# The border to the experts: fills of empty rows beside the puts, on two queues, the plan in memory of its own, weights ahead of rows

## The chip, the cores and the metric

The kernel runs on one core of a Trainium2 chip. The metric is the device time of one execution in microseconds (us). Engines are named as in the profile: PE (matrix products and transposes; PEld its weight loads), DVE, ACT, POOL (elementwise engines; POOL also issues the indirect DMAs) and SP (issues DMAs and computes nothing). An engine that issues a DMA does it in its own stream of instructions, in order; such rows carry a q (SPq, ACTq).

## The reference

A tensor x of 2 x 256 x 48 x 48 passes two layers. The first is a mix of local attention and convolutions. The second turns the picture into 2 x 2304 tokens of 256 numbers and runs a state-space token mixer, and behind it a mixture of experts. All is float32. The part that matters here is the mixture:

```python
xf = x.reshape(-1, D)
gate_logits = xf @ Wg + bg
top_w, top_i = jax.lax.top_k(gate_logits, TOP_K)          # 2 of 8 experts for each token
top_w = jax.nn.softmax(top_w, axis=-1)
w_dense = jnp.sum(jax.nn.one_hot(top_i, E, dtype=xf.dtype) * top_w[..., None], axis=1)
for e in range(E):
    h = jax.nn.gelu(xf @ W1[e] + b1[e], approximate=False)  # 256 -> 1024
    out = out + w_dense[:, e:e + 1] * (h @ W2[e] + b2[e])   # 1024 -> 256
```

and the result is added to the tokens (after their normalization, for the experts' input).

## The kernel before, in words

The kernel doesn't run all tokens through all experts. It sorts them: `xs` is a table in device memory with one part for each of the 8 experts (`PART` = 4608 + 256 rows) and a spare piece behind them. A row has 265 numbers: the token's 256 channels, its weights for the experts, and its number.

**The tail of the mixer.** While the mixer runs (`mamba`), each group of up to six chunks of 128 tokens is routed: DVE finds the two best experts and, from running counts, the row of each token in each expert's part. POOL then puts the rows: two indirect DMAs of 128 rows for a chunk, 72 in all (`put`, line 1630, `xs<-u,rows`). They are declared free of order among themselves, as a group named "rows". The last group's counts end in `self.taken`, one number for each expert. The order on PE, DVE, ACT and SP in this stage is written out by a planner (`Flow`) in the program; POOL's follows from the same plan.

**The border** (`experts`). `ends` (line 1730) is `taken` plus one: the first empty row of each part. `fill(e)` (line 1747) writes 256 rows of zeros with the number of a spare token there, since the experts work on tiles of 128 or 256 rows and the last tile of a part reaches past its tokens. The row is a register's value, loaded on the issuing engine by `value` (line 1711). `plan` (lines 1641 to 1708) works out on DVE, in some forty small instructions, which expert and which row each tile has. `fetch(i)` loads tile i: its rows `ex` (line 1758 for tile 0, line 1764 for others), the biases `bt` (line 1767) and the weights `wt` of 2 MB (line 1769). Tile 0 is always the first of expert 0, whose weights are loaded long before (`first_weights`). All these DMAs are issued by SP.

**The tiles.** There are 36 pair tiles of 256 rows and 4 single tiles of 128 that always run, and 4 more under a condition. For each: `turn` transposes the rows on PE (line 896, copied out on DVE, line 898) and takes out the weights of the tokens and their numbers; `up` makes the first product (line 1826) in eight chunks, each in one of four PSUM banks, with a Gelu on ACT (line 1830); `down` makes the second product, for pair tiles with seven products instead of eight (line 1864), for which `weight_sums` (lines 1800 to 1803, `ts`) and `hidden_sums` (lines 1812 to 1815, `ss`) make sums on DVE; `finish` scales the result on ACT and adds it to `acc` by an indirect DMA of POOL (line 1836). `run` goes over the tiles; at the end of tile i it fetches tile i + 3.

Outside the planner's part a scheduler of the framework orders the instructions of each engine when the program is built; what is wrapped in `keep_in_program_order` keeps its order. It also sets the waits: an instruction waits for every earlier one that it may conflict with in memory, unless both were declared free of order. Memory of a closed pool is given to later pools; the pools of `experts`, that of the plan among them, lie where the mixer's were.

Of the kernel before, what the change touches and what calls it, by code (L numbers as in the profile page):

```python
# [31 lines left out]
F32 = mybir.dt.float32  # L32
I32 = mybir.dt.int32
AF = mybir.ActivationFunctionType
# [3 lines left out]
P = 128  # L38
B, C, H, W = 2, 256, 48, 48
N = H * W  # L40
NH = C // P
# [29 lines left out]
E, HID = 8, 1024  # L71
NHC = HID // P

TR = 256
# [4 lines left out]
NROWS = E * PART + TR  # L79
XW = C + E + 1  # L80
WMAT = NH * HID + NHC * C
# [144 lines left out]
class Kernel:  # L226
# [1496 lines left out]
    def experts(self, ctx):  # L1723
        nc, ins = self.nc, self.ins
        self.psum(ctx, 4, 2)
        hp = self.pool("eh", 2, ctx)
        ew = self.pool("ew", 3, ctx)
        plan = self.pool("plan", 1, ctx)
        ends = plan.tile([P, E], I32, name="ends")
        nc.vector.tensor_scalar(ends, self.taken, 1.0, None, ALU.add)  # L1730
        sp = [mybir.EngineType.SP]
        fetched, turned, hidden, sums = {}, {}, {}, {}

        tiles = []

# [5 lines left out]
        usual = len(tiles)  # L1741
        tiles += [(1, i) for i in range(NUSUAL, NSINGLE)]

        def fill(e):
            row = self.value(ends[0:1, e : e + 1], sp, NROWS - TR)
            put = self.tc.keep_in_program_order(
                nc.sync.dma_start(
                    self.expert_rows(self.xs[bass.ds(row, TR), :]), self.none
                )
            )  # L1750
            self.tc.declare_no_dep(put.ins, group="fill", reason="every part of the table has its own")
            self.tc.add_to_no_dep_group("fill", put.ins)

        def fetch(i):
            halves, n = tiles[i]
            x = hp.tile([P, 2, XW], F32, tag="ex", name="ex", bufs=3)[:, :halves]
            if i == 0:
                self.tc.keep_in_program_order(nc.sync.dma_start(x, self.expert_rows(self.xs[0:TR, :])))
                fetched[i] = x, self.first_weights[:, :WMAT], self.first_weights[:, WMAT:]
                return  # L1760
            at = where[2 - halves]
            row = self.value(at[0:1, 0, n : n + 1], sp, NROWS - TR)
            part = self.value(at[0:1, 1, n : n + 1], sp, (E - 1) * P)
            nc.sync.dma_start(x, self.expert_rows(self.xs[bass.ds(row, halves * P), :]))

            bt = hp.tile([P, WCOL - WMAT], F32, tag="bt", name="bt", bufs=5)
            self.tc.keep_in_program_order(nc.sync.dma_start(bt, ins["We"][bass.ds(part, P), WMAT:]))
            wt = ew.tile([P, WMAT], F32, tag="wt", name="wt")
            self.tc.keep_in_program_order(nc.sync.dma_start(wt, ins["We"][bass.ds(part, P), :WMAT]))
            fetched[i] = x, wt, bt  # L1770

        def turn(i):

            halves = tiles[i][0]
            x, wt, bt = fetched[i]
            xt = hp.tile([P, NH, halves * P], F32, tag="ext", name="ext")
            self.transposes(
                xt.rearrange("p k q -> p (k q)"),
                [x[:, j, k * P : (k + 1) * P] for k in range(NH) for j in range(halves)], nc.vector.tensor_copy,
            )  # L1780
            own = hp.tile([P, halves, E], F32, tag="own", name="own")
            nc.vector.tensor_tensor(
                own, x[:, :, C : C + E], bcast(bt[:, NHC + C :], 1, [P, halves, E]), ALU.mult
            )
            weight = hp.tile([P, halves], F32, tag="weight", name="weight")
            nc.vector.tensor_reduce(weight, own, AX.X, ALU.add)
            token = hp.tile([P, halves], I32, tag="token", name="token", bufs=12)
            nc.vector.tensor_copy(token, x[:, :, XW - 1].bitcast(I32))
            turned[i] = xt, weight, token

        def weight_sums(i):


            if i >= len(tiles) or tiles[i][0] == 1:
                return
            w2 = fetched[i][1][:, NH * HID : NH * HID + NHC * C].rearrange("p (k h o) -> p k h o", k=NHC, h=2)
            b11, b12, b21, b22 = (w2[:, k * NHC // 2 : (k + 1) * NHC // 2, h] for k in range(2) for h in range(2))
            ts = hp.tile([P, 4, NHC // 2, P], F32, tag="ts", name="ts", bufs=1)
            t1, t2, t3, t4 = (ts[:, j] for j in range(4))
            nc.vector.tensor_sub(t1, b12, b11)  # L1800
            nc.vector.tensor_sub(t3, b22, b12)
            nc.vector.tensor_sub(t2, b22, t1)
            nc.vector.tensor_sub(t4, b21, t2)
            sums[i] = dict(b11=b11, b21=b21, b22=b22, t1=t1, t2=t2, t3=t3, t4=t4)
# [11 lines left out]
            sums[i] |= dict(a11=a11, a12=a12, a22=a22, s1=s1, s2=s2, s3=s3, s4=s4)  # L1816

        def up(i):
            rows = tiles[i][0] * P
            xt, wt, bt = turned[i][0], *fetched[i][1:]  # L1820
            w1 = wt[:, : NH * HID].rearrange("p (k o) -> p k o", k=NH)
            hid = hidden[i] = hp.tile([P, NHC, rows], F32, tag="hid", name="hid")
            for c in range(NHC):
                ps = self.bank()
                for k in range(NH):
                    nc.tensor.matmul(  # L1826
                        ps[:, :rows], lhsT=w1[:, k, c * P : (c + 1) * P], rhs=xt[:, k, :],
                        start=k == 0, stop=k == NH - 1,
                    )
                nc.scalar.activation(hid[:, c, :], ps[:, :rows], AF.Gelu, bias=bt[:, c : c + 1])  # L1830

        def finish(i, y, j):

# [6 lines left out]
            self.tc.add_to_no_dep_group(f"tile{i}", put.ins)  # L1840

        def down(i):
            wt, bt, hid = *fetched[i][1:], hidden[i]
            w2 = wt[:, NH * HID : NH * HID + NHC * C].rearrange("p (k o) -> p k o", k=NHC)
            b2 = bt[:, NHC : NHC + C]
            banks = self.ps2.tile([P, 2, 512], F32, tag="banks", name="po")
            if tiles[i][0] == 1:
                y = hp.tile([P, C], F32, tag="ey", name="ey", bufs=5)
                po = banks[:, 0, :C]
                for c in range(NHC):  # L1850
                    nc.tensor.matmul(po, lhsT=hid[:, c, :P], rhs=w2[:, c, :], start=c == 0, stop=c == NHC - 1)  # L1851
                nc.vector.tensor_add(y, po, b2)
                finish(i, y, 0)
            else:
                v = sums.pop(i)
                p = {}

                for n, (name, a, w) in enumerate((
                    (1, "a11", "b11"), (7, "s3", "t3"), (2, "a12", "b21"), (4, "a22", "t4"), (5, "s1", "t1"),
                    (6, "s2", "t2"), (3, "s4", "b22"),  # L1860
                )):
                    p[name] = banks[:, n // 4, n % 4 * P : (n % 4 + 1) * P]
                    for c in range(NHC // 2):
                        nc.tensor.matmul(p[name], lhsT=v[a][:, c], rhs=v[w][:, c], start=c == 0, stop=c == NHC // 2 - 1)  # L1864
                y0, y1 = (hp.tile([P, C], F32, tag="ey", name="ey", bufs=5) for _ in range(2))
                p1, u2, u3, u4 = (hp.tile([P, P], F32, tag=f"u{j}", name=f"u{j}", bufs=1) for j in range(4))
                add = nc.vector.tensor_add
                nc.scalar.copy(p1, p[1])  # L1868
                add(y0[:, :P], p[2], p1)
                add(u2, p[6], p1)  # L1870
                add(u3, p[7], u2)
                add(u4, p[5], u2)
                add(y1[:, :P], p[4], u3)
                add(y1[:, P:], p[5], u3)
                add(y0[:, P:], p[3], u4)
                for j, y in enumerate((y0, y1)):
                    add(y, y, b2)  # L1877
                    finish(i, y, j)
            del fetched[i], turned[i], hidden[i]

        fill(0)
        fetch(0)
        where, many = self.plan(plan)
        turn(0)
        for e in range(1, E):
            fill(e)
        fetch(1)
        fetch(2)
        weight_sums(0)

        def run(first, end):
            for i in range(first, end):
                up(i)
                if i + 1 < end:
                    turn(i + 1)
                if tiles[i][0] == 2:
                    hidden_sums(i)
                down(i)
                if i + 1 < end:
                    weight_sums(i + 1)  # L1900
                if i + 3 < end:
                    fetch(i + 3)
# [39 lines left out]
    def run(self):  # L1942
# [30 lines left out]
            self.layer0(l0)  # L1973
        up = self.pool("route", 1)
        self.taken = up.tile([P, E], F32, name="taken")
        nc.vector.tensor_copy(self.taken, self.c["base"])
        self.first_weights = self.pool("ew0", 1).tile([P, WCOL], F32, name="wt")
        nc.sync.dma_start(self.first_weights, self.ins["We"][0:P, :])
# [93 lines left out]
```

## Time and profile before

| | us |
|---|---|
| runs of before | 1396.8, 1399.08, 1402.14, 1402.41, 1402.56 |
| median | 1402.14 |
| the profiled execution | 1399.72 |
| its span (first to last instruction) | 1397.9 |
| PE busy | 1261.5 (90%) |
| DVE busy | 1015.5 (73%) |
| ACT busy | 789.3 (56%) |
| POOL busy | 531.6 (38%) |
| last put of rows begins | 826.21 |
| first product of tile 0 begins | 839.42 |
| first product of tile 1 begins | 857.67 |

Every time below is counted from the begin of the span. In a chain of waits a row has its start, its length and what ran; in a timeline a bracket gives the idle time of the engine before the instruction and what ended it. A row such as "SPq L1747 <- DMA ex<-xs: 1.9, 1, 1.9" says that SP's stream stood before line 1747 for 1.9 us in all, once, at the longest 1.9 us, until a DMA of `ex<-xs` landed.

### The profile page before, as it was taken

The page shows a single profiled execution, that of the slowest core. Times are in us where ns is not written, and L with a number is a line of the kernel's source. Part 1 is how long each engine was busy: PE and PEld are TensorE (multiplying, and loading weights), DVE is VectorE, ACT ScalarE, POOL GpSimd, SP SyncE. Part 2 cuts the span into 40 slices and gives each one's busy share as a digit, 9 for nine tenths or more (in the row PEclk, how much of TensorE's full clock was granted, in tenths as well). Part 3 has the DMA queues.
Part 4 walks back from the last instruction along what each step waited for, and adds up shares of the span by engine and source line. Part 5 has one row for each costly group of instructions (what it writes and reads, how often), then busy time and mean ns, then how long its engine had stood idle before and what let it go on. Part 6 is the DMA issues. An engine that isn't in the chain of part 4 may idle for free.

```text
span 1397.9 us, 23793 instructions
## 1 busy us (share of the span) xinstructions
PE 1261.5 (90%) x8144; PEld 1006.3 (72%) x8144; DVE 1015.5 (73%) x2638; ACT 789.3 (56%) x1932; POOL 531.6 (38%) x648
## 2 busy tenths in 40 slices
PE   4999999997999889898988709999999999999993
PEld 3566767666676566665656508999999999999992
DVE  5999999998789879799988635665565566556552
ACT  2688878887987676776876403333332333333332
POOL 4313030111366777868676840212221221222220
PEclk9999999998999999999999859999999999999997
DMA  8321313112323232333242128767665775676637
GB/s 287 105 92 44 122 59 106 37 55 75 105 66 96 85 102 90 117 92 124 82 129 88 54 94 289 230 184 235 211 217 178 239 233 181 217 235 207 188 81 278
DMA packets 101259, 199.55 MB, mean 143 GB/s; under 512 B 10491, under 2 KB 83788, under 8 KB 95692
## 3 DMA queue, kind: packets, MB, share of 16 engines
q1 hardware_dynamic: 83756, 171.57, 36.1%
q0 software_dynamic: 14400, 19.74, 7.3%
q10 hardware_dynamic: 2980, 6.69, 1.2%
q8 instruction: 66, 1.08, 0.3%
q14 instruction: 57, 0.47, 0.1%
HBM read 158.71 MB, written 44.18 MB: 145 GB/s over the span
## 4 chain that ended last, share of the span: by engine, by line
PE 51%; DVE 12%; DMA 4%; ACT 2%; POOL 2%; issue 2%; SPq 1%; another core or an unknown queue 0%; DVEq 0%; ACTq 0%; POOLq 0%
PE bank L1826 18%; PE po L1864 16%; PE bank L910 4%; PE zbank L910 2%; PE bank L1421 2%; PE bank L1403 2%; DVE xc L1107 2%; PE bank L1360 1%; POOL xs L1630 1%; PE bank L896 1%; DVE mt L1323 1%; DVE bc L1107 1%; PE po L1851 1%; PE bank L1341 1%; DMA cz<-bc 1%
## 5 line engine op out<-in xcount | busy, mean ns | idle before, releaser
L1836 POOL DMA_INDIRECT acc<-ey,token x76 | 118.7, 1561 | 422.4 <-ACT ey L1835 380.1
L1826 PE MATMUL bank<-ext,wt 128*128 128x256 f32 (+1 forms) x1280 | 271.5, 371 | 3.4 <-DMA wt<-in_We 2.6
L1826 PEld LDWEIGHTS bank<-ext,wt 128*128 128x128 f32 x1280 | 232.3, 191 | 32.5 <-DVE ey L1877 2.7
L1830 ACT ACTIVATE hid<-bank,bt 128x256 f32<-128x256 f32 (+1 forms) x312 | 143.2, 461 | 93.3 <-PE bank L1826 88.3
L1868 ACT COPY u<-po 128x128 f32<-128x128 f32 x36 | 9.6, 266 | 225.1 <-PE po L1864 225.1
L1864 PE MATMUL po<-ts,ss 128*128 128x128 f32 x864 | 108.2, 275 | 0.0
L1864 PEld LDWEIGHTS po<-ts,ss 128*128 128x128 f32 x864 | 102.3, 192 | 0.0
L586 DVE SCALAR_TENSOR_TENSOR x<-hid,w2r,x 128x1128 f32<-128x1128 f32 (+3 forms) x72 | 99.9, 1392 | 0.4 <-ACT hid L580 0.2
L910 PE MATMUL bank<-xn,win 128*128 128x387 f32 x240 | 94.7, 518 | 1.2 <-DVE lg L1446 1.0
L675 POOL COPY kp<-kp 128x10 f32<-128x10 f32 (+1 forms) x60 | 23.5, 392 | 189.0 <-DVE kp L668 189.0
L794 ACT ACTIVATE prob<-prob,top 128x308 f32<-128x308 f32 x144 | 78.1, 548 | 17.5 <-DVE top L783 17.1
L1315 ACT ACTIVATE mt<-mt,cum 128x128 f32<-128x128 f32 x288 | 87.4, 396 | 0.0
L1107 DVE SCALAR_TENSOR_TENSOR xc<-bank,vec,xc 128x384 f32<-128x384 f32 x144 | 85.1, 606 | 1.9 <-ACT xc L1096 1.7
L1800 DVE TENSOR_TENSOR ts<-wt 128x512 f32<-128x512 f32 x36 | 24.9, 692 | 81.2 <-PE po L1864 81.2
L1813 DVE TENSOR_TENSOR ss<-hid 128x512 f32<-128x512 f32 x36 | 24.9, 691 | 77.8 <-ACT hid L1830 77.8
L1630 POOL DMA_INDIRECT xs<-u,rows x72 | 71.9, 998 | 22.5 <-issue 16.7
L910 PE MATMUL zbank<-xn,win 128*128 128x384 f32 x192 | 75.8, 518 | 4.2 <-ACT z L1217 4.2
L1864 PE MATMUL po<-wt,hid 128*128 128x128 f32 x576 | 76.1, 275 | 0.0
L1421 PE MATMUL bank<-wout,y 128*128 128x264 f32 x288 | 72.4, 395 | 2.4 <-DVE ss L1436 1.9
L1864 PEld LDWEIGHTS po<-wt,hid 128*128 128x128 f32 x576 | 70.1, 192 | 0.1
L825 PE MATMUL bank<-pt,val 110*64 110x128 f32 (+1 forms) x864 | 69.4, 278 | 0.8 <-ACT pt L815 0.8
L800 ACT ACTIVATE prob<-prob,rden 128x308 f32<-128x308 f32 x144 | 67.7, 546 | 4.1 <-DVE rden L849 4.0
(293 smaller groups left out, 3010.1 us busy)
## 6 DMA issues: line engine op xcount, KB each, us to landing
wt<-in_We SPq DMA_DIRECT2D x39, 2048.0 KB
mt<-decays SPq DMA_DIRECT2D x36, 512.0 KB
ex<-xs SPq DMA_DIRECT2D x36, 265.0 KB
rd<-decays SPq DMA_DIRECT2D x68, 128.0 KB
val<-vtab SPq DMA_DIRECT2D x72, 110.0 KB
bt<-in_We SPq DMA_DIRECT2D x39, 136.0 KB
vraster<-vout SPq DMA_DIRECT2D x18, 256.0 KB
acc<-x SPq DMA_DIRECT2D x36, 128.0 KB
```

What stands on the lines that cost most here:

```text
L586: nc.vector.scalar_tensor_tensor(dst, src, w[:, k : k + 1], dst, ALU.mult, ALU.add)
L794: nc.scalar.activation(t, t, AF.Exp, bias=T["top", c][:, a : a + 1], scale=-1.0, accum_out=T["den", c][:, a : a + 1])
L825: nc.tensor.matmul(po[j * HD : (j + 1) * HD, :P], lhsT=T["val", c][:nk, i, a * HD : (a + 1) * HD], rhs=T["pt", key][:nk, j, i, :], start=i ...
L910: self.nc.tensor.matmul(ps, lhsT=lhs(k), rhs=rhs(k), start=k == 0, stop=k == NH - 1)
L1107: nc.vector.scalar_tensor_tensor(out(), T["bank", ("cv", at)][:, i : i + TB], wc[:, i : i + 1], out(), ALU.mult, ALU.add)
L1315: nc.scalar.activation(t, t, AF.Relu, bias=at_s, scale=-1.0)
L1421: nc.tensor.matmul(ps[:, : C + E], lhsT=T["y", c][:, m, :], rhs=self.l1["wout"][:, m, :], start=m == 0, stop=m == NZ - 1,)
L1630: ins = nc.gpsimd.indirect_dma_start(self.xs, bass.IndirectOffsetOnAxis(ap=of("rows")[:, i, q : q + 1], axis=0), T["u2", g][:, i, :], None,)
L1826: nc.tensor.matmul(ps[:, :rows], lhsT=w1[:, k, c * P : (c + 1) * P], rhs=xt[:, k, :], start=k == 0, stop=k == NH - 1,)
L1830: nc.scalar.activation(hid[:, c, :], ps[:, :rows], AF.Gelu, bias=bt[:, c : c + 1])
L1836: put = nc.gpsimd.indirect_dma_start(self.acc, bass.IndirectOffsetOnAxis(ap=token[:, j : j + 1], axis=0), y, None, compute_op=ALU.add)
L1864: nc.tensor.matmul(p[name], lhsT=v[a][:, c], rhs=v[w][:, c], start=c == 0, stop=c == NHC // 2 - 1)
```

## The change

- `plan`'s pool, with `ends`, is opened ahead of the mixer, so its memory isn't the mixer's any more.
- `fill` joins the group "rows" of the puts: fills and puts are declared free of order among one another. It takes the issuing engine: SP for expert 0, ACT for experts 1 to 7.
- `fetch` is split in `fetch_rows` and `fetch_weights`. For tiles 1 and 2 the weights are fetched ahead of the rows; for the others rows are first as before. The rows' DMA now keeps program order too.
- The order of the border becomes: fill 0 and tile 0's rows on SP, fills 1 to 7 on ACT, the plan, the turn of tile 0, weights and rows of tiles 1 and 2. Before, fills 1 to 7 were on SP between the turn of tile 0 and the fetch of tile 1.
- `weight_sums(0)` moves behind `up(0)`.

```diff
-        plan = self.pool("plan", 1, ctx)
+        plan = self.plans
...
-        def fill(e):
-            row = self.value(ends[0:1, e : e + 1], sp, NROWS - TR)
+        def fill(e, engine, kind):
+            row = self.value(ends[0:1, e : e + 1], [kind], NROWS - TR)
             put = self.tc.keep_in_program_order(
-                nc.sync.dma_start(
+                engine.dma_start(
                     self.expert_rows(self.xs[bass.ds(row, TR), :]), self.none
                 )
             )
-            self.tc.declare_no_dep(put.ins, group="fill", reason="every part of the table has its own")
-            self.tc.add_to_no_dep_group("fill", put.ins)
-
-        def fetch(i):
+            self.tc.declare_no_dep(put.ins, group="rows", reason="rows behind those of the expert's tokens")
+            self.tc.add_to_no_dep_group("rows", put.ins)
+
+        def fetch_rows(i):
             halves, n = tiles[i]
             x = hp.tile([P, 2, XW], F32, tag="ex", name="ex", bufs=3)[:, :halves]
+            row = self.value(where[2 - halves][0:1, 0, n : n + 1], sp, NROWS - TR) if i else 0
+            self.tc.keep_in_program_order(
+                nc.sync.dma_start(x, self.expert_rows(self.xs[bass.ds(row, halves * P) if i else slice(0, TR), :]))
+            )
+            rows[i] = x
+
+        def fetch_weights(i):
+            halves, n = tiles[i]
             if i == 0:
-                self.tc.keep_in_program_order(nc.sync.dma_start(x, self.expert_rows(self.xs[0:TR, :])))
-                fetched[i] = x, self.first_weights[:, :WMAT], self.first_weights[:, WMAT:]
+                weights[i] = self.first_weights[:, :WMAT], self.first_weights[:, WMAT:]
                 return
-            at = where[2 - halves]
-            row = self.value(at[0:1, 0, n : n + 1], sp, NROWS - TR)
-            part = self.value(at[0:1, 1, n : n + 1], sp, (E - 1) * P)
-            nc.sync.dma_start(x, self.expert_rows(self.xs[bass.ds(row, halves * P), :]))
+            part = self.value(where[2 - halves][0:1, 1, n : n + 1], sp, (E - 1) * P)
...
+        def fetch(i):
+            fetch_rows(i)
+            fetch_weights(i)
...
-        fill(0)
+        fill(0, nc.sync, mybir.EngineType.SP)
         fetch(0)
+        for e in range(1, E):
+            fill(e, nc.scalar, mybir.EngineType.Activation)
         where, many = self.plan(plan)
         turn(0)
-        for e in range(1, E):
-            fill(e)
-        fetch(1)
-        fetch(2)
-        weight_sums(0)
+        for i in (1, 2):
+            fetch_weights(i)
+            fetch_rows(i)
 
         def run(first, end):
             for i in range(first, end):
                 up(i)
+                if i == 0:
+                    weight_sums(0)
                 if i + 1 < end:
                     turn(i + 1)
...
         self.taken = up.tile([P, E], F32, name="taken")
+        self.plans = self.pool("plan", 1)
```

The rest of the diff carries the new names through `turn`, `weight_sums`, `up` and `down`.

More of the change, by code (lines that the diff above doesn't have):

```diff
@@ L1731, in experts @@
         sp = [mybir.EngineType.SP]
-        fetched, turned, hidden, sums = {}, {}, {}, {}
+        rows, weights, turned, hidden, sums = {}, {}, {}, {}, {}
         tiles = []
@@ L1769, in fetch @@
             self.tc.keep_in_program_order(nc.sync.dma_start(wt, ins["We"][bass.ds(part, P), :WMAT]))
-            fetched[i] = x, wt, bt
+            weights[i] = wt, bt
+        def fetch(i):
+            fetch_rows(i)
+            fetch_weights(i)
         def turn(i):
             halves = tiles[i][0]
-            x, wt, bt = fetched[i]
+            x, bt = rows.pop(i), weights[i][1]
             xt = hp.tile([P, NH, halves * P], F32, tag="ext", name="ext")
@@ L1795, in weight_sums @@
                 return
-            w2 = fetched[i][1][:, NH * HID : NH * HID + NHC * C].rearrange("p (k h o) -> p k h o", k=NHC, h=2)
+            w2 = weights[i][0][:, NH * HID : NH * HID + NHC * C].rearrange("p (k h o) -> p k h o", k=NHC, h=2)
             b11, b12, b21, b22 = (w2[:, k * NHC // 2 : (k + 1) * NHC // 2, h] for k in range(2) for h in range(2))
@@ L1818, in up @@
         def up(i):
-            rows = tiles[i][0] * P
-            xt, wt, bt = turned[i][0], *fetched[i][1:]
+            cols = tiles[i][0] * P
+            xt, wt, bt = turned[i][0], *weights[i]
             w1 = wt[:, : NH * HID].rearrange("p (k o) -> p k o", k=NH)
-            hid = hidden[i] = hp.tile([P, NHC, rows], F32, tag="hid", name="hid")
+            hid = hidden[i] = hp.tile([P, NHC, cols], F32, tag="hid", name="hid")
             for c in range(NHC):
@@ L1826, in up @@
                     nc.tensor.matmul(
-                        ps[:, :rows], lhsT=w1[:, k, c * P : (c + 1) * P], rhs=xt[:, k, :],
+                        ps[:, :cols], lhsT=w1[:, k, c * P : (c + 1) * P], rhs=xt[:, k, :],
                         start=k == 0, stop=k == NH - 1,
                     )
-                nc.scalar.activation(hid[:, c, :], ps[:, :rows], AF.Gelu, bias=bt[:, c : c + 1])
+                nc.scalar.activation(hid[:, c, :], ps[:, :cols], AF.Gelu, bias=bt[:, c : c + 1])
         def finish(i, y, j):
@@ L1842, in down @@
         def down(i):
-            wt, bt, hid = *fetched[i][1:], hidden[i]
+            wt, bt, hid = *weights[i], hidden[i]
             w2 = wt[:, NH * HID : NH * HID + NHC * C].rearrange("p (k o) -> p k o", k=NHC)
@@ L1878, in down @@
                     finish(i, y, j)
-            del fetched[i], turned[i], hidden[i]
-        fill(0)
+            del weights[i], turned[i], hidden[i]
+        fill(0, nc.sync, mybir.EngineType.SP)
         fetch(0)
+        for e in range(1, E):
+            fill(e, nc.scalar, mybir.EngineType.Activation)
         where, many = self.plan(plan)
         turn(0)
-        for e in range(1, E):
-            fill(e)
-        fetch(1)
-        fetch(2)
-        weight_sums(0)
+        for i in (1, 2):
+            fetch_weights(i)
+            fetch_rows(i)
         def run(first, end):
```

## The prediction

> **What bounds the kernel now.** I read the page first: TensorE is busy in nine tenths or more of nearly every slice, apart from the begin and the slices around 770 to 860 us, where the token mixer ends and the experts begin. So I asked for stretches on both sides of that border (columns: busy time and instructions of PE, its weight loads, DVE, ACT, POOL; then granted clock, DMA share, GB/s).
>
> ```profile
> 802.20:805.70 3.50, 0.60 (x4) 0.48 (x4) 2.25 (x19) 0.00 (x0) 2.88 (x3) 0.98 0.46 154
> 813.57:829.20 15.63, 0.00 (x0) 0.00 (x0) 0.90 (x7) 0.00 (x0) 10.55 (x11) 0.50 0.27 96
> 837.50:847.20 9.70, 8.87 (x32) 7.29 (x33) 2.33 (x10) 4.03 (x7) 0.00 (x0) 0.71 0.68 198
> 848.40:857.50 9.10, 6.69 (x61) 6.50 (x59) 5.34 (x18) 0.84 (x3) 0.00 (x0) 1.00 1.00 353
> 858.00:1358.00 500.00, 500.00 (x3393) 468.15 (x3392) 292.60 (x750) 177.09 (x417) 114.00 (x73) 1.00 0.66 208
> ```
>
> From 858 to 1358 PE is busy 500.00 of 500.00 us: whatever brings the second tile's start forward brings the end forward by as much, one for one. Before that PE stands still from 811 to 837.5. The chain of waits for the border says why:
>
> ```profile
> 826.21 2.95 DMA xs<-u,rows
> 829.58 0.17 DVE ends L1730
> ...
> 833.95 2.78 DMA ex<-xs
> 836.75 0.39 SPq L1747
> ...
> 842.97 4.13 DMA xs<-none
> 847.21 0.41 SPq L1764
> 847.84 0.36 SPq L1767
> 848.39 9.14 DMA wt<-in_We
> 857.67 7.14 PE bank L1826 x32
> ```
>
> The last put of tokens' rows lands at 829.2, only then is `ends` computed, then fill 0 goes (issued 831.15), then tile 0's rows (833.95, landed 836.73), then fills 1 to 7, then tile 1's rows and weights. What SP waited for, and PE's two starts in the timeline (start, length, last bracket: idle before):
>
> ```profile
> SPq L1764 <- DMA xs<-none: 2.5, 1, 2.5
> SPq L1758 <- DMA xs<-none: 2.2, 1, 2.2
> SPq L1747 <- DMA ex<-xs: 1.9, 1, 1.9
> ```
>
> ```profile
> 837.55 1.08 PE L896 MATMUL bank<-cst,ex 128*128 128x128 f32 x4 [26.94 <-DVE wherep L1704]
> 839.42 8.99 PE L1826 MATMUL bank<-ext,wt 128*128 128x256 f32 x32 [0.79 <-DVE ext L898]
> 841.56 1.28 ACT L1830 ACT_TABLE_LOAD   x1 [28.40 <-DMA xs<-none]
> 857.67 7.14 PE L1826 MATMUL bank<-ext,wt 128*128 128x256 f32 x32 [2.58 <-DMA wt<-in_We]
> ```
>
> The third waits row matters most: fill 1 was held until tile 0's rows had been read. A fill's row is a register's value, so the program must suppose that it overlaps `xs[0:TR]`. The change takes the order between fills and puts away, not this one: `fetch(0)` still stands ahead of fills 1 to 7.
>
> **Part 1, the plan's own memory, fill 0 beside the puts.** The counts `taken` are written at 813.7, the tail of that group's chain runs to 814.5; `ends` and the plan can follow at once. SP then issues fill 0 near 815.5, and only tile 0's rows still wait for the last put. SP's walk through its semaphores ran from 829.2 to 829.7, so I put that issue at 829.7 instead of 833.95: 4.25 us. The landing stays 2.78. PE began 0.8 us after the landing, with the last plan instruction (wherep) named; that plan is now long done, but some of the gap is PE's own nine semaphore steps of 0.05, so 0 to 0.77, I take 0.35. Tile 0's first product then starts at 839.42 - 4.6 = 834.8.
>
> **Part 2, weights ahead of rows.** SP issues tile 1's weights 1.2 us after tile 0's rows (as 847.21 to 848.39 now), at 830.9. They needed 9.14 us with DMA full; even 14 us would have them at 845, before PE is through with tile 0 (855.10 - 4.6 = 850.5). The 2.58 us in the bracket go. Sum of gains: 4.25 + 0.35 + 2.58 = 7.2.
>
> **Part 3, fills 1 to 7 on ACT.** These seven, with a register load each, leave SP (836.75 to 843.35 now) and stand in ACT's stream ahead of tile 0's Gelus (ACT has nothing else between 813.2 and 841.5). Held by tile 0's rows, they start at 832.5. ACT's load of a register took 0.46 (at `many`), its DMA issues a median of 0.40; with the register steps some 1.05 each, less the first load: ACT is free at about 839.5. Behind it waits the table load of 1.28, then the first Gelu (0.47): its bank is free at 841.3. PE has four banks; its fourth chunk of the first product ended 5.5 us after the start (844.9 now), so at 840.3. PE stalls 1.0 us. Between bounds: 0 if the fills go earlier, and at the worst issue lengths seen (0.89 on ACT, 1.26 on SP under a full DMA) 7 x 1.7 = 12 us, ACT free 844.4, stall 5.9. I take 1.2, as the medians are of the same instruction; DMA is loaded by the weights meanwhile.
>
> Tile 1's rows wait for the last fill. Alone, the seven took 10.35 us from first issue to last landing (836.75 to 847.1): 842.9; sharing with 2.2 MB of weights, up to 846. Rows land 2.8 to 3.8 later, 845.7 to 849.8. PE's stream turns tile 1 in the midst of tile 0's second product (851.14 now), at 847.7 with the stall above. Wait 0 to 2.1, I take 0.4. SP's queue behind tile 1's rows: tile 2's weights, issued by 848, landed by 858, needed at 866: covered by 8 us.
>
> The Trainium skill ("DMA: Bandwidth & Descriptors", Issuing engines are not separate DMA queues) speaks against this part: DMAs of all engines run on the same 16 DMA engines, so a second issuing engine saves only the time of issuing. No row of before has fills and weights in flight together; by that rule the fills would take their time from the weights, which have the cover named above.
>
> **Part 4, DVE's work beside the puts.** The plan, some 9 us of small DVE instructions, now runs while POOL makes eleven puts at 1.26 us each. Three puts beside DVE busy 2.25 of 3.5 us took 2.88 us, 0.96 each (first stretch above): the same as the 10.55 / 11 with DVE idle. The longest of all 72 is 1.24: bound 11 x 0.28 = 3.0 us, below nothing excluded. I take 0.1.
>
> The skill ("SBUF — State Buffer", Who interferes with whom) has DVE and GpSimd share a port pair under an exclusive lock, which a DVE instruction with two SBUF inputs contests with a GpSimd instruction that reads SBUF; if every two-input instruction of the plan held up a put for its whole length, an estimated 4.4 us would be lost instead of 0.1. The 0.96 beside a busy DVE speaks against it.
>
> **Part 5, moved at no cost.** The four `ts` sums of tile 0 move behind its first product: 2.6 us of DVE between the copy of `ext` (834.7) and the first half of `hid` (840.9), in an idle of 6.13 us; without that cover 2.6. Steady state: rows in program order on SP, an order that the trace already shows (rows, bt, then wt): nothing.
>
> **Sum.** 7.2 - 1.2 - 0.4 - 0.1 = 5.5 us. The profiled execution took 1399.72 us (span 1397.9, 1.8 around it), so 1394.2. The median of the five is 1402.14, 2.4 above it: 1396.6.
>
> **Rivals.** (a) Fills 1 to 7 don't wait for tile 0's rows and run beside the puts: DMA has three quarters free there, ACT is idle. Against it: the 1.9 us row. Part 3 costs nothing: gain 7.1, 1395.0; 0.21. (b) The gain turns into a new wait: ACT is held to 844 by issues at their worst, or tile 1's rows come 4 us late. Gain 0 to 3.5: 1400.4; 0.16. (c) Slower: ACT can't issue because its fills are served only behind the 2.2 MB of weights (to 840.5), then seven at 1.35: ACT free at 850, bank at 851.7, PE's last four chunks 3.5, second product 6.7: 861.9 against 857.67, so 1402.14 + 4.2 = 1406.3. It decides once ACT is free later than 845.5 (stall of 7). For it: a packet of weights held a DMA engine 151 ns, one of fills 55 (9.1 us x 16 / 965; 10.2 x 0.638 x 16 / 1904); against it: SP issued three weight tiles within 6 us with one slow issue; 0.10. (d) That nothing starts earlier, since `ends` still waits, would leave part 2: in (b).
>
> **Chances.** My forecast 0.53. A difference under 0.3% (4.2 us) can't be told from none here; a fifth of the forecast's own spread (gain 3 to 7) lies below it. Faster: 0.44 + 0.21 = 0.65; same: 0.09 + 0.16 = 0.25; slower 0.10. Range: the low end is (a) with all of PE's 0.77, 7.6, and the runs' spread around their median (some 3 us): 1391.5; the high end takes in (b) with no gain: 1402.
>
> **What would show it.** Right: `ends` near 814.5; tile 0's rows issued by 830; PE's first product at 834 to 835.5; no wait on `wt` at the second tile; fills 1 to 7 on ACT's queue from about 832.5, a table load near 840, PE waiting for a Gelu in the first product. Rival (a): those fills before 826. Wrong: puts longer than 0.96 (part 4), PE idle at tile 1's transposes for over 2 us, or any new wait behind 858.

## The result, and the profile after

The changed kernel took 1402.66 us (median) where the kernel before, run beside it on the same chips, took 1399.37: ratio 1.0022, 95% interval 1.0014 to 1.0030, so about 3.1 us slower. That is inside the 0.3% that the prediction called no change, but on the other side from its forecast: 5.5 us faster, 1396.6 from a median of 1402.14. The profiled execution of after took 1400.05 us, its span 1398.2 (before: 1399.72 and 1397.9).

The first half of the border went as forecast, the second did not. The chain of waits of after (start, length, what the end was waiting for; the lines from the second tile's start backwards):

```profile
828.76 2.78 DMA ex<-xs
831.56 0.41 ACTq L1747
...
839.07 8.91 DMA xs<-none
...
848.23 2.98 DMA ex<-xs
851.21 0.14 issue
851.34 1.09 PE bank L896 x4
```

Read it from the top. Tile 0's rows are read at 828.76 and landed at 831.54; at 831.56 fill 1 goes out, now on ACT's queue. The last fill is issued at 839.07 and needs 8.91 us, tile 1's rows leave at 848.23, and PE can turn that tile only at 851.34. The old chain, last put, fill 0, rows, fills, rows, has lost one link (fill 0) and kept the rest; what it kept has become longer. The timeline of the same stretch (start, length, instruction, bracket: idle before and what ended it):

```profile
825.35 0.96 POOL L1630 DMA_INDIRECT xs<-u,rows  x1 [0.30 <-issue]
828.76 0.38 SPq L1759 DMA_DIRECT2D ex<-xs  x1
830.25 0.35 SPq L1773 DMA_DIRECT2D wt<-in_We  x1
831.56 7.89 ACTq L1747 DMA_DIRECT2D xs<-none  x7
834.08 5.16 PE L1834 MATMUL bank<-ext,wt 128*128 128x256 f32 x16 [0.78 <-DVE ext L898]
839.92 1.28 ACT L1838 ACT_TABLE_LOAD   x1 [27.72 <-DVE wheres L1705]
841.74 3.72 PE L1834 MATMUL bank<-ext,wt 128*128 128x256 f32 x16 [2.51 <-ACT hid L1838]
851.34 1.09 PE L896 MATMUL bank<-cst,ex 128*128 128x128 f32 x4 [5.88 <-DMA ex<-xs]
852.22 1.92 PE L1872 MATMUL po<-wt,hid 128*128 128x128 f32 x8
```

The 2.58 us on `wt` at the second tile are gone. In their place stand two new waits of PE: 2.51 on a Gelu, behind ACT's seven issues, and 5.88 on tile 1's rows. And what follows the long wait is slow: four transposes take 1.09 instead of 0.60, eight products 1.92 instead of 1.06. The stretches name why (PE, its weight loads, DVE, ACT, POOL; granted clock, DMA share, GB/s):

```profile
842.00:845.40 3.40, 3.40 (x16) 2.70 (x15) 0.69 (x1) 2.21 (x6) 0.00 (x0) 1.00 1.05 196
845.50:851.30 5.80, 0.00 (x0) 0.00 (x0) 0.00 (x1) 0.47 (x1) 0.00 (x0) 0.95 0.41 99
851.34:853.00 1.66, 1.66 (x8) 1.66 (x9) 1.47 (x5) 0.00 (x0) 0.00 (x0) 0.50 0.70 246
855.00:859.00 4.00, 4.00 (x38) 4.00 (x37) 0.00 (x0) 0.00 (x0) 0.00 (x0) 1.00 0.94 366
```

PE stands still in the second row, and works at a granted clock of 0.50 in the third: the four transposes and the eight products together take 2.59 us (851.34 to 853.93) where the same ones take 1.36 at full clock in a run below (e2, 844.13 to 845.49), so 1.23 more. Measured from the begin of the last put (826.21 before, 825.35 after), the border adds up:

| step, from the last put's begin | before | after | change | forecast |
|---|---|---|---|---|
| tile 0's rows issued | +7.74 | +3.41 | -4.33 | -4.25 |
| tile 0's first product | +13.21 | +8.73 | -4.48 | -4.6 |
| wait of PE on `wt`, second tile | 2.58 | 0 | -2.58 | -2.58 |
| wait of PE on a Gelu | 0 | 2.51 | +2.51 | +1.2 |
| wait of PE on tile 1's rows | 0 | 5.88 | +5.88 | +0.4 |
| half clock behind it | 0 | 1.23 | +1.23 | 0 |
| second tile's first product | +31.46 | +34.02 | +2.56 | |

From the second row on the terms add up: -4.48 - 2.58 + 2.51 + 5.88 + 1.23 = +2.56.

### The profile page after: what moved, and what is told of

It reads as the page before. It is cut to its first block, busy times and chain, and to the rows that moved or that the text cites. A ratio compares the mean times of both kernels' runs of the same rounds, so it can differ in the third digit from the quotient of the medians.

```text
span 1398.2 us, 23768 instructions
## 1 busy us (share of the span) xinstructions
PE 1259.5 (90%) x8144; PEld 1004.4 (72%) x8144; DVE 1015.2 (73%) x2638; ACT 788.5 (56%) x1932; POOL 532.4 (38%) x648
## 3 DMA queue, kind: packets, MB, share of 16 engines
q10 hardware_dynamic: 4884, 8.59, 1.8%
## 5 line engine op out<-in xcount | busy, mean ns | idle before, releaser
L1808 DVE TENSOR_TENSOR ts<-wt 128x512 f32<-128x512 f32 x36 | 24.9, 692 | 89.0 <-PE po L1872 78.9
L1821 DVE TENSOR_TENSOR ss<-hid 128x512 f32<-128x512 f32 x36 | 24.9, 691 | 76.1 <-ACT hid L1838 76.1
```

## The experiments

**Theory:** the changes to the plan and to fill 0 gain what was forecast, and two things give it back. Fills 1 to 7 are still held by the read of tile 0's rows, and now share the DMA engines with 2.2 MB of weights that go ahead of them, so tile 1's rows come late for a PE that works in order; and ACT is held by seven issues. **Rivals:** it is only the place at which PE waits (tile 1's transposes now stand ahead of tile 0's second product); it is ACT's hold alone; it is the bytes of the fills, wherever they are put.

Every run's border, from the begin of its last put to the first product of the second and of the third tile (us), with its ratio to the kernel before:

| run | 2nd tile | 3rd tile | ratio (95%) |
|---|---|---|---|
| before | 31.46 | 45.13 | 1 |
| after | 34.02 | 47.62 | 1.0022 (1.0014 to 1.0030) |
| e1_fills_first | 28.45 | 42.05 | 0.9979 (0.9962 to 0.9996) |
| e2_rows_first | 26.99 | 40.69 | 0.9971 (0.9956 to 0.9986) |
| e3_turn_late | 36.11 | 52.84 | 1.0059 (1.0042 to 1.0076) |
| e4_fills_sp | 27.93 | 44.50 | 0.9986 (0.9968 to 1.0004) |
| e5_plan_only | 29.34 | 43.01 | 0.9973 (0.9955 to 0.9991) |
| e8_fill0_only | 27.38 | 42.50 | 0.9977 (0.9958 to 0.9995) |
| e10_rows_half | 24.67 | 38.37 | 0.9955 (0.9933 to 0.9977) |
| e11_first_half | 24.80 | 38.40 | 0.9955 (0.9936 to 0.9974) |
| e12_after_half | 27.69 | 41.29 | 0.9973 (0.9957 to 0.9989) |
| e13_sp_half | 24.87 | 38.58 | 0.9966 (0.9951 to 0.9982) |
| e14_first_half_sp | 24.62 | 38.22 | 0.9969 (0.9951 to 0.9987) |

The third tile's start, less 45.13, follows the change of the median to within about 2.6 us (e14: -6.9 against 0.0031 x 1398.69 = -4.3), so where two runs lie closer than that, their borders are compared and not their ratios. A border is that of one profiled execution. Behind the third tile's start all 13 executions are alike, 525.2 to 526.6 us to the end of the span; ahead of the border they differ, the last put begins between 824.10 (e2) and 832.67 (e8), and that is why borders are counted from it.

### The order of issue: e1, e2

e1 moves fills 1 to 7 ahead of tile 0's fetch, so that nothing reads `xs` before them; this builds the prediction's rival (a):

```diff
-        fetch(0)
         for e in range(1, E):
             fill(e, nc.scalar, mybir.EngineType.Activation)
+        fetch(0)
```

> Fills 1 to 7 (still on ACT) stand ahead of tile 0's rows in the program. Theory A, that the loss comes from fills held until tile 0's rows are read: the fills are issued by ACT near 814 to 822 beside the puts and land before the last put; no Gelu of tile 0 is held, PE doesn't wait at tile 1's transposes, and the second tile's product begins about 24.5 us after the last put's begin instead of 34.2 (before: 31.5): ratio to before 0.995. Theory B, that it is tile 1's rows queued behind 2 MB of weights: PE still waits at tile 1's transposes, gain over the changed kernel under 4 us, ratio about 0.999 to 1.0. Theory C, that fills and plan beside the puts stretch them: puts longer than 1.0 us each and the last one later by some us, ratio 0.998 or more.

PE has no wait left after its start: the second tile's line in e1's timeline carries no bracket. But the start is late, 28.45 behind the last put where theory A had 24.5:

```profile
834.31 0.38 SPq L1759 DMA_DIRECT2D ex<-xs  x1
855.22 7.07 PE L1834 MATMUL bank<-ext,wt 128*128 128x256 f32 x32
```

Its last put began at 826.77, so tile 0's rows leave 7.54 after it (after: 3.41). The chain of waits of e1 shows the put itself:

```profile
826.77 6.59 DMA xs<-u,rows
```

A put that needed 2.95 us to land now needs 6.59, behind fills of 1.9 MB on the same DMA engines (stretches 820.5 to 823 and 828 to 830 of e1):

```profile
820.50:823.00 2.50, 0.00 (x0) 0.00 (x0) 0.00 (x0) 0.00 (x0) 1.89 (x3) 0.50 1.13 238
828.00:830.00 2.00, 0.00 (x0) 0.00 (x0) 0.00 (x0) 0.00 (x0) 0.00 (x0) 0.50 1.15 224
```

The engines are full (share over 1) at under 240 GB/s. So the hold on fills 1 to 7 in after is the read by tile 0, and taking it away gives 3.1 us against before, not the 7.1 that the rival (a) reckoned: "three quarters free" was true of the stretch before, but the fills fill it.

e2 keeps after's place for the fills and swaps two issues on SP, tile 1's rows ahead of its weights:

```diff
         for i in (1, 2):
-            fetch_weights(i)
             fetch_rows(i)
+            fetch_weights(i)
```

> Only the order of weights and rows of tiles 1 and 2 goes back to rows first, so no weights are in flight while the fills are written. If sharing the DMA engines with tile 1's weights is what made the seven fills take 16.4 us from first issue to last landing: they land in 11 to 12 us, tile 1's rows arrive near 845.5 instead of 851.2, PE's wait at the transposes falls from 5.9 to under 1 us, and the second tile begins about 6 us earlier than in the changed kernel, held by its weights (issued near 843.5, landed near 852.5): ratio 0.997. If ACT's own issuing is slow instead: the fills land as late as before and the weights later still, the second tile begins near 862, ratio 1.004.

As expected. From the first issue to the last landing the seven fills take 10.34 us (830.85 to 841.19), as in before (10.35), where after took 16.4 (831.56 to 847.98). First e2's chain, then its timeline:

```profile
837.05 4.14 DMA xs<-none
```

```profile
830.85 6.58 ACTq L1747 DMA_DIRECT2D xs<-none  x7
839.67 3.72 PE L1834 MATMUL bank<-ext,wt 128*128 128x256 f32 x16 [0.75 <-ACT hid L1838]
844.13 0.63 PE L896 MATMUL bank<-cst,ex 128*128 128x128 f32 x4 [0.75 <-DMA ex<-xs]
851.09 7.17 PE L1834 MATMUL bank<-ext,wt 128*128 128x256 f32 x32
```

Three things shrink at once when the weights step back: the wait on tile 1's rows (5.88 to 0.75), ACT's seven issues (7.89 to 6.58) and with them the wait on the Gelu (2.51 to 0.75). The clock stays full, and the weights, though last, are there when PE wants them. "Weights ahead of rows" was the part of the change that cost; without it after's other parts win 0.3%.

### The engine and PE's place: e4, e3

e4 leaves the order and issues the fills from SP:

```diff
         for e in range(1, E):
-            fill(e, nc.scalar, mybir.EngineType.Activation)
+            fill(e, nc.sync, mybir.EngineType.SP)
```

> Fills 1 to 7 are issued by SP, at their place behind tile 0's rows, so ACT is free and tile 1's weights go out behind the fills. PE's 2.5 us in tile 0's first product are gone if ACT's queue made them. The scheduler puts tile 1's transposes behind tile 0's second product here, so the wait there should be gone too: tile 0 ends near 849.8, the weights of tile 1 (issued near 838.5, fills before them) land near 847 to 849, the second tile begins near 851: ratio 0.996. If ACT's hold isn't the cause of the 2.5 us, they stay.

```profile
833.95 9.37 PE L1834 MATMUL bank<-ext,wt 128*128 128x256 f32 x32 [0.78 <-DVE ext L898]
836.10 1.28 ACT L1838 ACT_TABLE_LOAD   x1 [24.11 <-PE bank L1834]
853.06 10.04 PE L1834 MATMUL bank<-ext,wt 128*128 128x256 f32 x32 [2.74 <-DVE ext L898]
```

The table load is done early, at 836.10, and the first product runs through: the 2.51 us were ACT's hold. The second tile starts 6.1 us earlier than in after. But this edit is not a test of ACT alone: in SP's stream tile 1's weights now go out behind the fills (839.31, the last fill at 837.78), and the built order of PE changed too (tile 1's transposes stand behind the whole second product). And the third tile gains little: behind the wait of 2.74 PE works at half clock, and the product takes 10.04 instead of some 7.1. So the ratio, 0.9986, misses the 0.996 that was expected.

e3 moves PE's place alone: tile 1's turn behind tile 0's second product.

```diff
-                if i + 1 < end:
+                if i and i + 1 < end:
                     turn(i + 1)
...
             down(i)
+                if i == 0:
+                    turn(1)
```

> Only the turn of tile 1 moves behind tile 0's second product, on PE; on DVE tile 1's weights-of-tokens still stand ahead of tile 0's second, third and fourth sums of hidden values. PE starts the second product at once after the first (no 5.9 us wait), does four of seven products, and then waits some 3 us for DVE, which stands for tile 1's rows until 851: the second tile begins about 3 us earlier than in the changed kernel, ratio 0.9995 to 1.001. If only PE's order mattered: 6 us earlier, ratio 0.998.

This fell far from the expectation: the slowest of all, 1.0059.

```profile
852.28 2.05 PE L1872 MATMUL po<-ts,ss 128*128 128x128 f32 x16 [2.48 <-DVE ss L1821]
859.95 0.17 DVE L1790 TENSOR_TENSOR own<-ex,bt 128x16 f32<-128x16 f32 x1 [6.28 <-DMA ex<-xs]
862.45 10.20 PE L1834 MATMUL bank<-ext,wt 128*128 128x256 f32 x32 [6.79 <-DVE ext L898]
```

DVE is in order too. Its small instructions on tile 1's rows, then on tile 2's, stood in its stream ahead of `ss` (tile 0's second product) and of the copy of tile 1's `ext`; PE waits for those 2.48 and 6.79 us, and then runs at half clock again. So "PE's place" as the sole cause falls: when rows come late, moving one waiting instruction moves the wait to the next engine; and in e2 above and e12 below PE's place is that of after and most of the wait on the rows is gone.

### The parts of the gain: e5, e8

e5 is the kernel before with the plan's own memory and nothing else:

```diff
-        plan = self.pool("plan", 1, ctx)
+        plan = self.plans
...
+        self.plans = self.pool("plan", 1)
```

> The kernel before with one part of the change alone: the plan's memory of its own. Fills still wait for the puts, on SP, in the old order. Theory A (each part is worth what it takes out of the chain between the last put and the second tile): only the way from the last put to fill 0 gets shorter, since ends and its register are ready: 1.5 us; second tile's product 30 us after the last put's begin instead of 31.5; ratio 0.999. Theory B (plan beside the puts slows POOL): puts over 1.0 us, ratio 1.001 or more.

```profile
832.49 0.42 SPq L1747 DMA_DIRECT2D xs<-none  x1
858.85 7.14 PE L1826 MATMUL bank<-ext,wt 128*128 128x256 f32 x32 [1.13 <-DMA wt<-in_We]
```

Fill 0 leaves 2.98 after the last put (829.51) instead of 4.94, so 2.0 us come from the plan; tile 0's rows still wait for fill 0. The ratio, 0.9973, is better than expected, with the expected 0.999 inside its interval; its border (-2.1 at the third tile) agrees with the expectation.

e8 is e4 and e2 together, that is, of the whole change only the plan, the free fill 0, the split of the fetch and the moved `weight_sums(0)` are left: fills on SP, rows ahead of weights.

> The changed kernel without its two queues and without weights ahead of rows: fills 1 to 7 on SP behind tile 0's rows, then rows, then weights of tiles 1 and 2. Left are the plan's memory and fill 0 beside the puts. Theory A (these two parts carry the gain, the other two lose it again): tile 0's product at 8.8 us after the last put's begin, no wait for a Gelu, none over 2 us at tile 1's transposes, second tile's product at 26 to 27 us after the last put's begin, held by its weights; ratio 0.996 to 0.997, as good as or better than with rows first and fills on ACT. Theory B (ACT's queue is needed): the fills' issue on SP makes rows and weights of tile 1 later by their 6.6 us, second tile at 31 us or later, ratio 1.0.

```profile
860.05 8.59 PE L1834 MATMUL bank<-ext,wt 128*128 128x256 f32 x32 [2.49 <-DMA wt<-in_We]
```

The second tile's start is as in e2 (27.38 against 26.99 after the put), with a wait of 2.49 on the weights in it, as before had one of 2.58; the third tile's is 1.8 later, 1.4 of it from a product of 8.59 instead of 7.14. e8 and e2 differ in the program in the fills' queue alone, but the built order of PE differs with it (tile 1's transposes stand in the midst of the second product in e8, ahead of it in e2). So in these two executions ACT's queue, with that order, is 0.4 us ahead at the second tile and 1.8 at the third, most of that through the clock; the ratios, 0.9977 and 0.9971, don't tell the two kernels apart. The border, 27.38, is a little above the 26 to 27 that were expected.

### The bytes: e11, e10, e12, e13, e14

A rest of up to 128 rows of an expert goes into a single tile and a longer one into a pair, so the tiles of experts 1 to 7 never reach more than 127 rows past their tokens, while each fill writes 256. Five kernels write 128 for these (expert 0 keeps 256); e10 is e2 with it, e11 is e1, e12 is after, e13 is e8, and e14 is e1 with all fills on SP:

```diff
+            n = P if e else TR
...
-                    self.expert_rows(self.xs[bass.ds(row, TR), :]), self.none
+                    self.expert_rows(self.xs[bass.ds(row, n), :]), self.none[:, : n // P]
```

> Fills 1 to 7 ahead of tile 0's rows, as in the first experiment, but of 128 rows each instead of 256 (experts 1 to 7 never reach further past their tokens). There the DMA engines were full from 816 to 831 and the last put landed 6.6 us after its begin instead of 2.95. If the bytes of the fills do that: half of them take some 4 us less, the last put lands within 3.5 us again, tile 0's rows go out 4 us after the last put's begin instead of 7.5, second tile's product at 25 to 25.5 us instead of 28.4; ratio 0.9955. If it is something else that fills and puts together do (order among queues, not bytes): no change, 0.998.

> Rows ahead of weights, fills on ACT behind tile 0's rows, as in the second experiment, with fills 1 to 7 of 128 rows each. ACT still issues seven, so PE's wait for the Gelu in tile 0 stays (0.7 to 0.8 us); the fills land some 2 us earlier (their issue sets it), rows and weights of tile 1 go out 2 us earlier, and the second tile starts as soon as tile 0 is done, 26 us after the last put's begin instead of 27: ratio 0.9962.

> The changed kernel with fills 1 to 7 of 128 rows instead of 256, nothing else. Theory A (tile 1's rows are late because the fills' packets share the DMA engines with tile 1's weights): the last fill lands 4 to 5 us after its issue instead of 8.9, tile 1's rows arrive about 21 us after the last put's begin instead of 25.9, PE waits 1 to 2 us at tile 1's transposes instead of 5.9 and keeps its clock; PE's wait for ACT's Gelu stays at 1.5 to 2.5 us, since seven fills are still issued; second tile's product 27.5 us after the last put's begin instead of 34.0; ratio to before 0.997. Theory B (the landing of a fill is late for another reason than its bytes): the wait of 5.9 us stays, ratio 1.002.

e11 as expected. Its chain of waits holds the put before the last:

```profile
827.72 2.96 DMA xs<-u,rows
```

It lands in 2.96 us, tile 0's rows leave 3.56 after the begin of the last put (828.98), and PE has no wait left after its start. e10 is the fastest of all, with e11: 1393.17 us (median) beside 1400.32 of before, ratio 0.9955 (0.9933 to 0.9977). Its first and second tile:

```profile
834.81 9.59 PE L1835 MATMUL bank<-ext,wt 128*128 128x256 f32 x32 [0.78 <-DVE ext L898]
850.97 7.17 PE L1835 MATMUL bank<-ext,wt 128*128 128x256 f32 x32
```

e12 keeps all of the change and only halves the bytes. First its chain, then its timeline:

```profile
841.60 4.29 DMA xs<-none
```

```profile
834.35 7.59 ACTq L1748 DMA_DIRECT2D xs<-none  x7
844.24 3.72 PE L1835 MATMUL bank<-ext,wt 128*128 128x256 f32 x16 [1.99 <-ACT hid L1839]
849.10 0.63 PE L896 MATMUL bank<-cst,ex 128*128 128x128 f32 x4 [1.14 <-DMA ex<-xs]
```

From first issue to last landing 11.5 us instead of 16.4, and the wait on tile 1's rows 1.14 instead of 5.88, at full clock behind it. Half the bytes in the same order on the same queues turn +2.5 us at the third tile into -3.8: it was the shared engines that made the rows late. ACT's hold stays (1.99).

> Rows ahead of weights, all fills on SP, fills 1 to 7 behind tile 0's rows and of 128 rows each: the version with rows first and short fills, without ACT's queue. If the second queue is worth nothing: the second tile's product 24.7 to 25.5 us after the last put's begin, as with ACT's queue (24.7), ratio 0.9955 to 0.996. If ACT's queue is worth SP's time: later by up to 2 us and a wait on wt, ratio 0.997.

> Short fills ahead of tile 0's rows, all on SP's queue, beside the puts. SP has nothing else to do there, so if only the bytes and the order matter, it is the same as with ACT's queue (second tile's product 24.8 us after the last put's begin, ratio 0.9955); ACT's table load is as early. If two queues get the fills a greater share of the DMA engines beside the puts, it differs: the last put would land earlier or later by over 0.5 us.

With the small fills the queue makes no difference that shows: e13 (SP) 24.87 against e10 (ACT) 24.67 at the second tile, e14 (SP) 24.62 against e11 (ACT) 24.80. The ratios, 0.9966 and 0.9969, are above the 0.9955 that was expected, but it lies inside both intervals. This is what the Trainium skill states ("DMA: Bandwidth & Descriptors", Issuing engines are not separate DMA queues): a second issuing engine saves time of issuing only. Here not even that shows: the seven issues took 6.15 us on ACT's queue in e10 and 6.26 on SP's in e13, and neither kept PE waiting for more than 0.8.

## Why the prediction was wrong, by its steps

**Part 1 was right.** Tile 0's rows were issued 4.33 us earlier (4.25 forecast), its first product 4.48 (4.6). e5 shows that 2.0 of it come from the plan's memory alone.

**Part 2 was right as to its gain and wrong as to its price.** The 2.58 us went. But the prediction looked for the weights' cover only ("even 14 us would have them at 845") and let them go ahead of the rows; e2 without this part is 7.0 us better at the second tile.

**Part 3 holds the step that failed:** "Wait 0 to 2.1, I take 0.4" for tile 1's rows. It was 5.88, outside both bounds, with 1.23 of half clock behind it. Both ends of the wait were off. The landing of the last fill was bounded at 846; it came at 847.98. The prediction cited the rule that the weights and fills share 16 engines, and then put the loss on the weights, "which have the cover named above", with 3.1 us for the fills as their bound; e2 and e12 show that the fills lost, 6 us of it. The other end, "PE's stream turns tile 1 in the midst of tile 0's second product (851.14 now), at 847.7 with the stall above", was read from the trace of before; PE came at 845.46. Of the 3.8 us beyond the bound of 2.1, 1.4 are the rows (landed at 851.21, where the latest allowed was 849.8), 2.2 are PE's early coming, and 0.1 lies between the landing and PE's start. The built order of PE's stream had changed. In before the transposes of tile 1 stood behind 26 products of tile 0's second product; in after, as shown above (851.34), they stand ahead of all of them:

```profile
850.92 0.39 PE L1864 MATMUL po<-ts,hid 128*128 128x128 f32 x2
851.14 0.60 PE L896 MATMUL bank<-cst,ex 128*128 128x128 f32 x4
851.58 0.83 PE L1864 MATMUL po<-ts,hid 128*128 128x128 f32 x6
```

Why the order was built so was not found out. In e3 and e4 the transposes stand behind the whole second product, in e5 and e8 in its midst: the place moves with small edits, and with it where a late transfer hurts.

In the same part, ACT's hold was the right mechanism with a term too small: seven issues of 7.89 us and a wait of 2.51, inside the bounds of 0 to 5.9, where 1.2 was taken. ACT came to its table load at 839.92 (839.5 forecast) and the bank was free at 841.74 (841.3); and PE, starting at 834.08 and not 834.8, stood there at 839.23 already (840.3).

**Part 4 was right:** the eleven puts took 0.96 to 1.02 us each, and from the first one's begin to the last one's it was 12.74 us instead of 12.64, the 0.1 that was forecast. Only five of them ran beside the plan, whose part for the pair tiles ended at 818.40; no lock of a shared port shows.

**Part 5 cost nothing, at another place:** the four `ts` sums of tile 0 ran from 828.49 to 831.11, in DVE's idle ahead of tile 0's turn, and from the second tile's start to the third's it was 13.60 us (13.67 in before).

**Rival (b), "the gain turns into a new wait", was what happened,** by its second branch (tile 1's rows late), and beyond its end: it gave a gain of 0 to 3.5. (a) fell twice: fills 1 to 7 did start at 831.56, held as the third waits row of before said, and when e1 frees them they spoil the puts. (c) did not occur; ACT could issue and was at its table load at 839.92, far from 850. The loss came by (b)'s way.

## What to carry to other kernels

A transfer that is moved up must be priced by what it takes from those that share the DMA engines and are wanted sooner, above all when the thing it overtakes has no cover; that its own deadline is met says nothing. Where a wait is shifted, ask on which in-order stream the waiting instruction will stand and what is queued behind it, and don't read that place from the trace of another build. And before transfers are reordered, see whether their bytes are needed: with halved fills, whether ahead of tile 0's rows or behind them and from whichever queue, the second tile began 24.6 to 24.9 us behind the last put, and even the order that lost 2.5 us at the third tile won 3.8.

## What the runs showed of the hardware

**The clock after short waits.** A wait of 2.58 us in before left the granted clock at 1.00 (a product of 7.14), and so did one of 2.51 in after and one of 2.48 in e3; one of 2.49 in e8 led to 8.59, one of 2.74 in e4 to 10.04 and one of 6.79 in e3 to 10.20; shorter ones, up to 1.99 (e12), left it full. So around 2.5 us the length alone doesn't decide. The records change the granted clock in steps of 3.413 us: the half-clock stretches behind these waits last 3.41 us in after and e8, 6.83 in e4, 10.24 in e3. The Trainium skill ("TensorE: Matmul & The Clock Gate", What's actually happening) tells of a free-running window of this length that has to be idle; the multiples agree, but 2.49 us is shorter than a window and did cost. Counted by these steps (the eight below are at full clock themselves), PE's busy time sorts the cases:

| run, step of its clock records (us) | PE busy in it | clock of the next step |
|---|---|---|
| after, 847.27 to 850.68 | 0.00 | 0.50 |
| e3, 854.95 to 858.37 | 0.71 | 0.50 |
| e8, 856.16 to 859.57 | 1.40 | 0.50 |
| e4, 848.66 to 852.07 | 1.56 | 0.50 |
| after, 843.86 to 847.27 | 1.60 | 1.00 |
| e3, 848.13 to 851.54 | 1.67 | 1.00 |
| before, 853.37 to 856.78 | 1.72 | 1.00 |
| e12, 840.25 to 843.67 | 1.99 | 1.00 |

So what a wait of 2.5 us costs here went with how it fell into these steps: when it left PE busy for 1.56 of a step's 3.41 us or less, the next step was at half clock. That is a reading of eight steps and not a test; no run moved a wait within a step on purpose, and 1.56 and 1.60 are close for products whose ends are modelled. The begin of e4's half-clock stretch (the second row holds the first 3.94 us of the product of 10.04):

```profile
850.30:853.06 2.76, 0.02 (x1) 0.00 (x0) 2.73 (x13) 1.00 (x2) 0.40 (x1) 0.82 1.00 429
853.06:857.00 3.94, 3.94 (x9) 3.20 (x10) 2.44 (x4) 0.59 (x2) 2.90 (x2) 0.50 1.07 399
```

**The fills' rate.** Seven fills of 256 rows took 10.35 us from first issue to last landing alone, 16.4 beside a tile's weights; beside the puts they filled the DMA engines at 224 to 238 GB/s, where the stretches with the weights' transfers saw 366 to 429 (after from 855, e4 from 850.3). A DMA share of 0.27, as before had beside the puts, says little of how much of such traffic still fits.
